# Casting x in a cross-attention kernel: reading in order and writing into two halves in turn, against reading at a step of two columns

## The chip, the cores and the metric

The kernel runs on one core of one Trainium2 chip. The metric is the device time of one execution in microseconds (us). A core has four compute engines here: PE (matrix products, with weight loads shown apart as PEld), DVE, ACT and POOL. SP issues DMAs. SBUF is the working memory that DMAs fill and all engines read; PE writes its results into eight PSUM banks (the tile `banks`).

## The reference, cut to what matters

```python
B, C, N = (32, 256, 1024)
x_q = jnp.einsum('oc,bcn->bno', w_qk, y)
x_k = jnp.einsum('oc,bcn->bon', w_qk, x)
x_v = jnp.einsum('oc,bcn->bon', w_v, x) + b_v[None, :, None]
energy = jnp.einsum('bnc,bcm->bnm', x_q, x_k)
attention = jax.nn.softmax(energy, axis=-1)
attention = attention / (1e-07 + attention.sum(axis=1, keepdims=True))
x_r = jnp.einsum('bcn,bnm->bcm', x_v, attention)
x_r = jax.nn.relu(jnp.einsum('oc,bcn->bon', w_t, x - x_r) + b_t[None, :, None])
return x + x_r
```

All is float32. For each of 32 batches a 1024 x 1024 score matrix is made, normalised along its rows by the softmax and then along its columns by a sum, and used to mix the values.

## The kernel before, in words

**Three forms.** PE works on operands of type fp32r, a rounded fp32. To keep fp32 precision every operand is held in three forms, HIGH, LOW and REST: HIGH is the value as a cast to fp32r rounds it, REST is what the cast lost, and for x LOW is HIGH / 4096 plus REST. A product of two operands is then three products of like forms, added in a bank. So x becomes `xf`, y becomes `yf`, the key side of the scores becomes `gf`, the softmax rows become `ef` (four buffers in turn), and the values become `uf`. The weights are multiplied together beforehand (`gw`, `vw`, `tw`).

**Layout of the moving operand.** A row of 1024 columns of `xf`, `gf` or `ef` is stored in two halves: the first 512 places hold the even columns, the other 512 the odd ones. PE reads its moving operand through `woven` (L275): element 0 of the first half, element 0 of the second, element 1 of the first, and so on, so that columns come in their natural order. `parted` (L278) views a row as [2 halves][512], `in_turn` (L284) views a row in natural order as [even or odd][512], at a step of two columns.

**Loading x (`load_x`, L372).** For each of the two blocks of 128 channels of a batch: SP's DMA brings x into `xr` in natural order; ACT casts it into `xf` HIGH; POOL subtracts HIGH from `xr` into REST; ACT scales HIGH into LOW; POOL's DMA adds REST to LOW. The first batch has its own code (`first_x`, four casts of 512 columns) and is not touched by the change. So `load_x` runs for 31 batches and issues 62 casts; the profile shows them as ACT `CAST xf<-xr 128x1024`.

**One batch.** Eight row tiles of scores (`energy`, L494, tokens E0 to E7): PE makes a 128x1024 tile in a pair of banks from `yf` and `gf` (shown as `MATMUL banks<-gf,yf`, twelve to a tile, six for each half of 512 columns); DVE takes the row's minimum (`TENSOR_REDUCE small<-banks`), ACT the exponential in the banks, DVE the reciprocal of the row's sum; then for each half of 512 columns ACT scales the row into `ef` HIGH (`ACTIVATE ef<-banks,small`), DVE makes REST (`SCALAR_TENSOR_TENSOR ef<-banks,small,ef`) and DVE adds the row to the running column sums `acc`. Only then may PE write that half of the pair again. ACT and POOL make LOW. `attention` (L549, tokens A0 to A7) multiplies `uf` by `ef` into four banks kept for the whole batch, again twelve products. Around them stand the values of the batch (V, v), the product of x with w_t (W), the keys of the next batch (k), the column sums (S), the output (O), the loads of y (Y) and `load_x` of the next batch (X).

**What sets the order.** The tokens of a batch stand in strings written by hand, for the steady batches

```python
STEADY = (
    "W0^ E0^ E1 E2 W1^ V1^ E3 Y2 A0 E4 A1 E5 A2 X E6 A3 E7 Y3 S A4 A5 v0 k1 A6 A7 k0 O"
)
```

They fix PE's order. For the other engines a planner (`Plan`, L19) estimates a cost and a due time for every instruction (for ACT: `columns / 1200 + 0.1` us, L243) and orders each engine's queue by them before the kernel is built; an engine then works through its queue strictly in that order. An instruction's cost in the plan depends on its number of columns alone, not on how they are read or written.

Of the kernel before, what the change touches and what calls it, by code (L numbers as in the profile page):

```python
# [184 lines left out]
def kernel(  # L185
# [12 lines left out]
    B, C, N = x.shape  # L198
# [12 lines left out]
    HIGH, LOW, REST = range(FORMS)  # L211
# [24 lines left out]
    pe, dve, act, pool, sync = (InOrder(g) for g in (nc.tensor, nc.vector, nc.scalar, nc.gpsimd, nc.sync))  # L236
# [6 lines left out]
    def on_act(columns, reads, writes, trace, more=0.0):  # L243
        plan.add("act", columns / 1200 + 0.1 + more, 0.09, reads, writes, trace)
# [11 lines left out]
    def on_pool(columns, reads, writes, trace):  # L256
        busy = columns * 2.25 / 1024 + 0.12
        plan.add("pool", busy, 0.0, reads, writes, trace, port=busy)

    def by_sync(landing, reads, writes, trace, early=0.0):  # L260
        plan.add("sync", 0.4, landing, reads, writes, trace, early=early)
# [4 lines left out]
    def by_pool(landing, reads, writes, trace):  # L266
        plan.add("pool", 1.2, landing, reads, writes, trace)

    def value(v):
        return v.bitcast(F32)  # L270
# [7 lines left out]
    def parted(v):  # L278
        return v.rearrange("p (a b) -> p a b", a=2)
# [4 lines left out]
    def in_turn(v):  # L284
        return v.rearrange("p (b a) -> p a b", a=2)

    def accumulate(into, from_):
        pool.dma_start(into, from_, accum_op=ALU.add)
# [9 lines left out]
    xf = one.tile([P, FORMS, KC, N], F32R, name="xf")  # L298
# [4 lines left out]
    xr = one.tile([P, KC, N], F32, name="xr")  # L303
# [65 lines left out]
    def x_names(j, k, halves=range(MH)):  # L369
        return [f"xf{j}{k}{h}" for h in halves]  # L370

    def load_x(b):  # L372
        for k in range(KC):

            def of(k=k):
                raw = [f"xr{k}{h}" for h in range(MH)]
                by_sync(5.0, ["yr"] if b == 1 else [], raw, lambda: sync.dma_start(xr[:, k], x[b, ts(k, P)]))
                on_act(N, raw, x_names(HIGH, k), lambda: act.copy(parted(xf[:, HIGH, k]), in_turn(xr[:, k])))
                on_pool(
                    N, raw + x_names(HIGH, k), x_names(REST, k),  # L380
                    lambda: pool.tensor_tensor(
                        parted(xf[:, REST, k]), in_turn(xr[:, k]), parted(value(xf[:, HIGH, k])), ALU.subtract
                    ),
                )
                on_act(
                    N, x_names(HIGH, k), x_names(LOW, k),
                    lambda: act.mul(xf[:, LOW, k], value(xf[:, HIGH, k]), 1.0 / UP),
                )
                by_pool(
                    8.2, x_names(LOW, k) + x_names(REST, k), x_names(LOW, k),  # L390
                    lambda: accumulate(value(xf[:, LOW, k]), value(xf[:, REST, k])),
                )

            of()
# [572 lines left out]
```

## Time and profile before

| what | value |
|---|---|
| median of three runs | 1881.09 us (1876.34 to 1881.65) |
| the profiled execution's own time | 1882.61 us |
| span of its instructions | 1880.7 us |
| mean granted TensorE clock | 0.998 |
| the 62 casts of x on ACT | 93.6 us of ACT's 1484.8 us |

The profile is of one execution. A row of the groups shows an instruction's output and inputs by the program's tile names, the shape, the count, then the busy time in us and the mean of one in ns, and the idle time of its engine just ahead of it with what ended that. All instructions have line 231, the helper that records them, so they are told apart by tiles. A row of a timeline shows the start in us, the time that the merged row takes, the engine and instruction, how many there are (x), and in brackets the idle time before it. Consecutive instructions of an engine overlap a little at their ends. A row of the waits shows the total in us, how often, and the longest.

### The profile page before, as it was taken

Reading aid. Unit: us, or ns where it says so; the run is one execution under the profiler, and the core shown is the slowest. Engines: PE = TensorE matmul, PEld = TensorE weight load, DVE = VectorE, ACT = ScalarE, POOL = GpSimd, SP = SyncE. Lnnn points to the kernel's source line nnn. Section 1 sums busy time; section 2 is a strip of 40 time slices with the busy share of each in tenths; the row PEclk is TensorE's granted clock in tenths of the full one; section 3 lists DMA queues with packets and bytes.
Section 4 is the critical chain, followed back from the end, with each engine's and each line's share of the span. In section 5 each row is a group of like instructions: output and inputs, shape, how many; then the busy total and the mean of one; then the engine's idle time right before and its main releaser. Section 6 shows DMA issues by size and latency. Waiting matters only on the chain.

```text
span 1880.7 us, 24352 instructions
## 1 busy us (share of the span) xinstructions
PE 1855.6 (99%) x8494; PEld 1597.4 (85%) x8494; DVE 1493.0 (79%) x2106; ACT 1484.8 (79%) x1936; POOL 1541.4 (82%) x773
## 2 busy tenths in 40 slices
PE   8999999999999999999999999999999999999998
PEld 7888888888888888888888888888888888888887
DVE  6787777887778878878777787777887877877878
ACT  6788777897777987778877789777797777887775
POOL 4788888888788888788888888888888788888777
PEclk9999999999999999999999999999999999999999
DMA  6666766667667667666676666666767666667652
GB/s 187 137 154 169 178 157 157 162 163 178 160 154 170 154 183 173 152 153 162 167 180 157 157 160 165 175 160 152 174 152 184 169 154 151 170 165 177 150 119 79
DMA packets 128651, 301.88 MB, mean 161 GB/s; under 512 B 12688, under 2 KB 47120, under 8 KB 128528
## 3 DMA queue, kind: packets, MB, share of 16 engines
q1 hardware_dynamic: 92272, 200.45, 34.4%
q0 software_dynamic: 35680, 99.10, 31.0%
q8 instruction: 66, 1.08, 0.2%
q10 hardware_dynamic: 576, 0.79, 0.1%
q14 instruction: 57, 0.47, 0.1%
HBM read 167.38 MB, written 67.11 MB: 125 GB/s over the span
## 4 chain that ended last, share of the span: by engine, by line
PE 33%; ACT 28%; DVE 14%; DMA 11%; issue 8%; POOL 4%; SPq 1%; DVEq 0%; POOLq 0%; ACTq 0%
PE banks L231 33%; ACT ef L231 10%; DMA blocks<-turned 6%; ACT banks L231 5%; DVE ef L231 5%; ACT xf L231 5%; DMA yr<-blocks 4%; DVE acc L231 4%; ACT xe L231 3%; ACT uf L231 3%; POOL ef L231 2%; DVE small L231 2%; ACT z L231 1%; SPq L231 1%; DVE parts L231 1%
## 5 line engine op out<-in xcount | busy, mean ns | idle before, releaser
L231 PE MATMUL banks<-gf,yf 128*128 128x512 f32 x3072 | 705.5, 381 | 8.5 <-DMA yf<-yf 2.8
L231 POOL TENSOR_TENSOR ef<-ef 128x1024 fp32r<-128x1024 f32 x256 | 640.5, 2516 | 79.8 <-DVE acc L231 35.4
L231 PE MATMUL banks<-ef,uf 128*128 128x512 f32 x3072 | 694.7, 379 | 1.1 <-POOL ef L231 0.6
L231 PEld LDWEIGHTS banks<-gf,yf 128*128 128x128 f32 x3072 | 576.2, 189 | 107.5 <-DVE ef L231 24.9
L231 PEld LDWEIGHTS banks<-ef,uf 128*128 128x128 f32 x3072 | 580.2, 189 | 85.1 <-POOL ef L231 1.4
L231 DVE TENSOR_REDUCE small<-banks 128x1 f32<-128x1024 f32 x256 | 312.5, 1221 | 174.1 <-PE banks L231 174.1
L231 DVE SCALAR_TENSOR_TENSOR ef<-banks,small,ef 128x512 fp32r<-128x512 f32 x512 | 366.5, 742 | 48.5 <-ACT ef L231 47.6
L231 ACT ACTIVATE ef<-banks,small 128x512 fp32r<-128x512 f32 x512 | 335.5, 706 | 4.1 <-DVE acc L231 0.6
L231 DVE SCALAR_TENSOR_TENSOR acc<-banks,small,acc 128x512 f32<-128x512 f32 x448 | 319.6, 743 | 5.7
L231 ACT ACTIVATE banks<-banks,small 128x1024 f32<-128x1024 f32 x256 | 281.8, 1101 | 23.2 <-DVE small L231 23.0
L231 ACT ACTIVATE ef<-ef 128x1024 fp32r<-128x1024 f32 x256 | 276.7, 1081 | 1.2
L231 ACT ACTIVATE gf<-banks 128x1024 fp32r<-128x1024 f32 x64 | 65.4, 1023 | 261.7 <-PE banks L231 259.8
L231 POOL TENSOR_TENSOR z<-z,xe 128x1024 f32<-128x1024 f32 (+1 forms) x64 | 149.1, 2345 | 68.2 <-DVE z L231 65.7
L231 POOL TENSOR_TENSOR uf<-yr,uf 128x1024 fp32r<-128x1024 f32 x64 | 152.2, 2377 | 57.4 <-ACT uf L231 57.1
L231 PE MATMUL banks<-xf,vw 128*128 128x512 f32 x768 | 183.4, 383 | 7.5 <-DVE ef L231 6.7
L231 PE MATMUL banks<-xf,gw 128*128 128x512 f32 x768 | 177.3, 380 | 1.1 <-DVE xf L231 0.7
L231 PE MATMUL banks<-xf,tw 128*128 128x512 f32 x774 | 176.5, 378 | 0.9 <-DVE banks L231 0.9
L231 PEld LDWEIGHTS banks<-xf,vw 128*128 128x128 f32 x768 | 142.6, 189 | 38.2 <-DVE ef L231 19.2
L231 PEld LDWEIGHTS banks<-xf,gw 128*128 128x128 f32 x768 | 144.7, 189 | 23.5 <-ACT acc L231 1.1
L231 PEld LDWEIGHTS banks<-xf,tw 128*128 128x128 f32 x774 | 145.4, 189 | 22.1 <-DVE banks L231 1.3
L231 POOL TENSOR_TENSOR uf<-turned,uf 128x1024 fp32r<-128x1024 f32 x64 | 154.9, 2420 | 8.5 <-ACT uf L231 6.2
L231 POOL TENSOR_TENSOR xf<-xr,xf 128x1024 fp32r<-128x1024 f32 x62 | 149.3, 2429 | 1.0 <-ACT xf L231 1.0
(68 smaller groups left out, 1633.8 us busy)
## 6 DMA issues: line engine op xcount, KB each, us to landing
yr<-in_ctx_dram SPq DMA_DIRECT2D x64, 512.0 KB, 4.3
blocks<-turned SPq DMA_DIRECT2D x256, 128.0 KB, 3.2
yf<-in_ctx_dram POOLq DMA_DIRECT2D x63, 512.0 KB, 6.1
yf<-yf POOLq DMA_DIRECT2D x63, 512.0 KB, 7.4
xo<-in_x_dram SPq DMA_DIRECT2D x62, 512.0 KB, 4.4
xr<-in_x_dram SPq DMA_DIRECT2D x62, 512.0 KB, 4.8
xf<-xf POOLq DMA_DIRECT2D x62, 512.0 KB, 6.7
out_dram<-z SPq DMA_DIRECT2D x62, 512.0 KB, 4.1
```

Source lines behind the costliest of these rows:

```text
L231: self.last = getattr(self.engine, name)(*args, **kwargs)
```

## The change

The cast into `xf` HIGH in `load_x` keeps its source, its destination and its 1024 columns, and visits them in another order. Before, it goes through the first half of the destination and then the second, contiguous in writing, and reads every other column of `xr`. After, it reads `xr` column by column and writes them to the first half and the second half in turn, so that each write is 512 places away from the one before. Both sides of the instruction become [512][2] where they were [2][512]. POOL's subtraction behind it, the set-up's casts and the plan are as they were.

```diff
                 by_sync(5.0, ["yr"] if b == 1 else [], raw, lambda: sync.dma_start(xr[:, k], x[b, ts(k, P)]))
-                on_act(N, raw, x_names(HIGH, k), lambda: act.copy(parted(xf[:, HIGH, k]), in_turn(xr[:, k])))
+                on_act(N, raw, x_names(HIGH, k), lambda: act.copy(
+                    xf[:, HIGH, k].rearrange("p (a b) -> p b a", a=2), xr[:, k].rearrange("p (b a) -> p b a", a=2)
+                ))
                 on_pool(
```

## The prediction

> **What bounds the kernel now.** I read the page of the profile first, then ACT's groups by shape, the waits, and last the timeline of each engine around one pair of the casts that the change edits.
>
> ```profile
> span 1880.7 us, 24352 instructions
> ...
> PE 1855.6 (99%) x8494; PEld 1597.4 (85%) x8494; DVE 1493.0 (79%) x2106; ACT 1484.8 (79%) x1936; POOL 1541.4 (82%) x773
> ```
>
> PE is busy 99% of the span, so the end moves only if PE does less or stands still less. The change takes nothing from PE's work. The question is whether ACT, through this cast, makes PE stand still. PE's waits name one large releaser:
>
> ```profile
> PEld banks L231 <- DVE ef L231: 44.8, 100, 1.6
> ...
> PE banks L231 <- DVE ef L231: 8.6, 17, 1.2
> ```
>
> These are a hundred short waits of PE's weight loads on DVE's step of the softmax, some three in each of 32 batches. One of the three is tied to the cast. This is the timeline of one batch in the middle, first ACT, then DVE, then PE with its weight load:
>
> ```profile
> 797.87 0.68 ACT L231 ACTIVATE ef<-banks,small 128x512 fp32r<-128x512 f32 x1
> 798.43 3.02 ACT L231 CAST xf<-xr 128x1024 fp32r<-128x1024 f32 x2
> 801.36 0.68 ACT L231 ACTIVATE ef<-banks,small 128x512 fp32r<-128x512 f32 x1
> 801.95 1.08 ACT L231 ACTIVATE banks<-banks,small 128x1024 f32<-128x1024 f32 x1
> ```
> ```profile
> 795.88 0.15 DVE L231 RECIPROCAL small<-small 128x1 f32<-128x1 f32 x1
> ...
> 799.83 1.22 DVE L231 TENSOR_REDUCE small<-banks 128x1 f32<-128x1024 f32 x1
> 802.08 0.75 DVE L231 SCALAR_TENSOR_TENSOR ef<-banks,small,ef 128x512 fp32r<-128x512 f32 x1 [1.04 <-ACT ef L231]
> ```
> ```profile
> 798.71 2.75 PE L231 MATMUL banks<-ef,uf 128*128 128x512 f32 x12
> 801.30 3.15 PE L231 MATMUL banks<-gf,yf 128*128 128x512 f32 x12
> 804.29 2.75 PE L231 MATMUL banks<-ef,uf 128*128 128x512 f32 x12
> 806.88 2.75 PE L231 MATMUL banks<-gf,yf 128*128 128x512 f32 x12
> ```
> ```profile
> 802.89 1.16 PEld L231 LDWEIGHTS banks<-gf,yf 128*128 128x128 f32 x6 [0.53 <-DVE ef L231]
> ```
>
> Read it backwards. A group of twelve products usually shows 2.75 us; the one from 801.30 shows 3.15, because its second six had to wait: 0.53 us in the weight loads, of which 3.15 - 2.75 = 0.40 us is lost on PE. They waited for DVE's ef at 802.08 to 802.83, which reads the bank that they overwrite. DVE had been idle 1.04 us, waiting for ACT's ef of 801.36. That ef is the second half of a tile whose first half ran at 797.87; the reciprocal that both need was there at 796.03. Between the halves stand the two casts, 3.02 us, on an engine that had no gap. So the chain is: two casts, ACT ef, DVE ef, PE.
>
> The rows repeat in the same form from the second batch that loads to the last but one:
>
> ```profile
> 105.37 3.02 ACT L231 CAST xf<-xr 128x1024 fp32r<-128x1024 f32 x2
> ...
> 1725.13 3.02 ACT L231 CAST xf<-xr 128x1024 fp32r<-128x1024 f32 x2
> ```
> ```profile
> 109.82 1.16 PEld L231 LDWEIGHTS banks<-gf,yf 128*128 128x128 f32 x6 [0.53 <-DVE ef L231]
> ...
> 1729.58 1.16 PEld L231 LDWEIGHTS banks<-gf,yf 128*128 128x128 f32 x6 [0.53 <-DVE ef L231]
> ```
>
> These are the first and the last of 29. The first and the last loading batch have another order.
>
> **The change part by part.** One instruction is edited, issued 62 times, two to a batch that loads. Plan, order, queues and DMAs stay. Only the duration of the cast can change, on its read side and on its write side.
>
> *What the strided read costs now.* ACT's groups by shape (count, then busy time and mean ns of one):
>
> ```profile
> L231 ACT CAST xf<-xr 128x1024 fp32r<-128x1024 f32 x62 | 93.6, 1555 | 0.0
> ...
> L231 ACT CAST yf<-yr 128x1024 fp32r<-128x1024 f32 x64 | 69.4, 1084 | 0.0
> ...
> L231 ACT ACTIVATE gf<-banks 128x1024 fp32r<-128x1024 f32 x64 | 65.4, 1023 | 261.7 <-PE banks L231 259.8 <-DVE sc L231 1.9
> ...
> L231 ACT CAST uf<-turned 128x1024 fp32r<-128x1024 f32 x32 | 33.9, 1060 | 0.7 <-DMA turned<-blocks 0.7
> ```
>
> The cast of x takes 1555 ns, casts of the same size that read in order 1084 and 1060. So reading SBUF at a step of two costs about 0.49 us. It is not the step alone: gf reads the PSUM banks at the same step in 1023 ns. Nor does the step cost as much when PE is quiet. In the set-up the cast in halves takes 725 ns beside 614 for a half in order, 0.11 more instead of the 0.25 that half of 0.49 would be; and in the first batch one full cast falls on a pause of PE and takes 1.34:
>
> ```profile
> L231 ACT CAST xf<-xr 128x512 fp32r<-128x512 f32 x4 | 2.7, 725 | 0.0
> L231 ACT ACTIVATE yf<-yf 128x512 fp32r<-128x512 f32 x3 | 1.7, 614 | 0.0
> ```
> ```profile
> 48.10 1.41 DVE L231 SCALAR_TENSOR_TENSOR ef<-banks,small,ef 128x512 fp32r<-128x512 f32 x2 [0.27 <-ACT ef L231]
> 48.53 1.34 ACT L231 CAST xf<-xr 128x1024 fp32r<-128x1024 f32 x1
> 48.90 3.10 PEld L231 LDWEIGHTS banks<-gf,yf 128*128 128x128 f32 x15 [0.59 <-DVE ef L231]
> 48.91 3.29 PE L231 MATMUL banks<-gf,yf 128*128 128x512 f32 x14 [0.18 <-DVE ef L231]
> ```
>
> I take the extra 0.49 us to be the strided read beside PE's reads of SBUF. The edit removes it, since the new read is in order.
>
> *What the scattered write will cost.* No ACT row of the trace writes SBUF element by element into two places. The lower bound is the 1060 ns of the uf cast, which writes in runs of 64; below the 1023 of gf I see no reason to go. For the upper bound the nearest rows are DVE's small sums: the first reads and writes at a step of five columns, the second is in order.
>
> ```profile
> L231 DVE TENSOR_REDUCE parts<-parts 32x32 f32<-32x32 f32 x96 | 19.7, 205 | 1.9
> ...
> L231 DVE TENSOR_REDUCE sc<-sc 32x32 f32<-32x32 f32 x32 | 5.6, 175 | 1.1
> ```
>
> That is 30 ns more for 32 elements, 0.94 ns an element. Laid wholly on the write of 1024 elements it gives 1.06 + 0.96 = 2.02 us. So the new cast lies between 1.06 and 2.02 us. I take 1.06, for two reasons. First, what slowed the read was PE reading beside it, and every product of PE writes into banks, never into SBUF: on the write side PE is no rival. Second, PE itself takes its moving operand from the two halves in turn, element by element, with the very step of the new write, and the timeline above shows no price: groups of twelve start 2.59 us apart (804.29 and 806.88), 216 ns for 512 columns.
>
> The Trainium skill has a rule that speaks against this change: "SBUF — State Buffer", section Specifications (TRN2), says that SBUF is kept in 16-byte lines, that full bandwidth needs at least two hits to a line, and that each step to a new line costs. By it the old read (two fp32 columns to a line) should be free and the new write (a new line at each element) should pay; the trace disagrees on the first (1555 against 1084) and, for PE's reads, on the second (216 ns at a new line for each column). The page gives no size, so the sum by it is the slower rival below.
>
> *What becomes of the time.* With 1.06 each, the two casts shorten by 2 x (1.555 - 1.06) = 0.99 us. ACT's ef moves up by as much, DVE's ef too, since DVE sat idle 1.04 us before it; PE needs only 0.53 of it. What is late next: DVE's TENSOR_REDUCE ends at 801.05, so its ef could end at 801.80, and PE reaches its second six products at about 802.6 (801.30 + 6 x 0.216). No stall is left there; half of the gain is unused. POOL does not see it: its own queue holds the next use of xf until 800.40.
>
> ```profile
> 798.05 2.40 POOL L231 TENSOR_TENSOR ef<-ef 128x1024 fp32r<-128x1024 f32 x1 [0.86 <-ACT ef L231]
> 800.40 4.81 POOL L231 TENSOR_TENSOR xf<-xr,xf 128x1024 fp32r<-128x1024 f32 x2
> ```
>
> The sum: 29 x 0.40 = 11.6 us. In the first loading batch DVE waited 0.27 us for an ef behind a single cast (48.10, above) and PE for DVE: 0.27. In the last one POOL waited 0.23 us for the cast and PE later 0.44 for POOL: 0.23.
>
> ```profile
> 1780.53 2.42 POOL L231 TENSOR_TENSOR xf<-xr,xf 128x1024 fp32r<-128x1024 f32 x1 [0.23 <-ACT xf L231]
> ...
> 1787.69 1.13 PE L231 MATMUL banks<-ef,uf 128*128 128x512 f32 x4 [0.44 <-POOL ef L231]
> ```
>
> Together 12.1 us. The profiled execution took 1882.6 us, so 1870.5; the median of the three runs lies 1.5 below the profiled time, so 1869.0. The other stalls of PE on DVE's ef come before the cast in each batch, from a chain that starts at PE's own products, and I leave them as they are.
>
> **The rivals.** *Slower: the write pays more than the read saves.* The place is the same; the point from which it decides is a cast of 1.555 us. Above it the stall grows by twice the excess in each batch, without slack, since ACT, DVE and PE already wait for each other in a row there. At 2.02 us: 29 x 2 x 0.465 = 27.0, and about 1 more in the two other batches, so 1881.1 + 28 = 1909. For it: DVE's strided small sums, and that a write of single elements into two places can't be gathered into wider ones. The page's rule on lines asks for this outcome. Against it: PE's reads in turn. Chance 0.33.
>
> *No change.* Either the price moves from the read to the write and the cast stays within 0.09 us of 1.555 (62 x 0.09 = 5.6 us, the bound of 0.3%), or the instruction pays for its inner run of two elements on both sides; or PE's gap stays although ACT is early. Against the last: DVE's idle 1.04 us ends with ACT's ef and nothing else. About 1881. Chance 0.13.
>
> *Faster*, as summed: any cast below about 1.30 us gives the whole 12 us, since 0.5 us for the pair is enough. Chance 0.54.
>
> **How the numbers follow.** The forecast is 1869.0. A difference of 0.3% (5.6 us) is about what a measurement of this kernel can tell from no change; the three runs spread over 5.3 us. The low end is the fastest of them less the gain, 1876.3 - 12.1 = 1864. Faster and no change hold 0.67, so the range must reach into the slower case, to its worked end of 1909 and a little over: 1912. The likeliest case's own range is 1864 to 1873. Faster 0.54, same 0.13, slower 0.33.
>
> **What would show it.** Right: the group of the cast near 1.06 us; the pair on ACT's timeline 2.0 instead of 3.02; DVE's ef behind it without its 1.04 of idle time; the group of twelve after it 2.75 instead of 3.15; PE's waits on DVE's ef down from 100 by about 29, and by 29 x 0.53 = 15 us. Wrong: a cast of 1.6 us or more, with DVE's idle time before ef longer and PE's group over 3.15; or a cast near 1.06 and the span unmoved, which would mean that another wait took the stall's place.

## The result, and the profile after

The changed kernel takes 1901.54 us (median of 4 runs, 1899.08 to 1905.83), the kernel before 1878.71 (median of 4 runs, the three shown and one more): a ratio of 1.0124 with a 95% interval of 1.0094 to 1.0155. It is slower, by about 23 us. The profiled executions differ by as much: 1905.83 against 1882.61 us.

The groups of ACT by shape show the edited instruction first (count, busy us, mean ns, idle time before it):

```profile
L231 ACT CAST xf<-xr 128x1024 fp32r<-128x1024 f32 x62 | 122.5, 2080 | 0.0
L231 ACT CAST yf<-yr 128x1024 fp32r<-128x1024 f32 x64 | 70.2, 1097 | 0.0
```

The cast takes 2080 ns where it took 1555, while the other casts are within 2% of what they were. The edit did what it says, and it cost 0.53 us a cast. These are the timelines of ACT, DVE, PE and PE's weight loads around one pair of casts, to be read as before from the bottom up:

```profile
866.98 0.69 ACT L231 ACTIVATE ef<-banks,small 128x512 fp32r<-128x512 f32 x1
867.55 3.94 ACT L231 CAST xf<-xr 128x1024 fp32r<-128x1024 f32 x2
871.27 0.68 ACT L231 ACTIVATE ef<-banks,small 128x512 fp32r<-128x512 f32 x1
871.84 1.09 ACT L231 ACTIVATE banks<-banks,small 128x1024 f32<-128x1024 f32 x1
```
```profile
868.95 1.22 DVE L231 TENSOR_REDUCE small<-banks 128x1 f32<-128x1024 f32 x1
871.98 0.75 DVE L231 SCALAR_TENSOR_TENSOR ef<-banks,small,ef 128x512 fp32r<-128x512 f32 x1 [1.82 <-ACT ef L231]
```
```profile
867.83 2.75 PE L231 MATMUL banks<-ef,uf 128*128 128x512 f32 x12
870.42 1.46 PE L231 MATMUL banks<-gf,yf 128*128 128x512 f32 x6
872.79 1.56 PE L231 MATMUL banks<-gf,yf 128*128 128x512 f32 x6 [0.92 <-DVE ef L231]
874.19 2.75 PE L231 MATMUL banks<-ef,uf 128*128 128x512 f32 x12
```
```profile
872.79 1.16 PEld L231 LDWEIGHTS banks<-gf,yf 128*128 128x128 f32 x6 [1.32 <-DVE ef L231]
```

It is the same chain. ACT's second half of the ef tile starts 871.27 - 867.55 = 3.72 us after the first cast; before it was 801.36 - 798.43 = 2.93. DVE's idle time before its ef rose from 1.04 to 1.82, the weight loads' wait from 0.53 to 1.32. PE's group starts 870.42 and the next one 874.19, 3.77 us apart instead of the 2.99 of before (801.30 to 804.29). Each of these moved by 0.78 or 0.79 us. It is the sign that the prediction named for being wrong: a cast above 1.6 us, a longer idle time of DVE before its ef, and more than 3.15 us for PE's group. Over the span, PE's waits on DVE's ef grew from 44.8 and 8.6 us to

```profile
PEld banks L231 <- DVE ef L231: 67.9, 101, 1.7
...
PE banks L231 <- DVE ef L231: 36.2, 45, 1.3
```

To add up what PE loses, I took from the trace the start of every product and counted what two neighbours are further apart than 0.216 us, if it is over 0.05 us, in the 29 batches with a pair of casts: from the first cast of a batch to 12 us after it ("behind the pair"), and in the 12 us ahead of the next pair. The table has the sums in us, with all kernels of this study; the last six are explained further down.

```
kernel               behind the pair   ahead of the next   time, median us
before                    11.5               12.4             1879.2
changed                   34.6               12.7             1901.5
one of two changed        22.6               12.9             1891.0
in order on both sides     0.0               12.5             1869.7
runs of two                0.0               12.7             1869.4
runs of eight              0.0               12.3             1869.3
half moved up, before      7.0               14.7             1879.0
half moved up, changed    31.4               12.5             1904.0
```

The change added 34.6 - 11.5 = 23.1 us behind the pairs. Over the whole execution the same count gives 41.9 us before and 65.2 us after, 23.3 more, so nothing worth naming was added elsewhere. That is the whole loss.

### The profile page after: what moved, and what is told of

Read it like the earlier page. It is cut to its first block, busy times and chain, and to the rows that moved or that the text cites. A ratio compares the mean times of both kernels' runs of the same rounds, so it can differ in the third digit from the quotient of the medians.

```text
span 1904.1 us, 24352 instructions
## 1 busy us (share of the span) xinstructions
PE 1854.6 (97%) x8494; PEld 1597.0 (84%) x8494; DVE 1493.3 (78%) x2106; ACT 1510.7 (79%) x1936; POOL 1547.3 (81%) x773
## 4 chain that ended last, share of the span: by engine, by line
PE 41%; ACT 25%; DVE 13%; DMA 9%; issue 8%; POOL 3%; SPq 1%; DVEq 0%; POOLq 0%; ACTq 0%
PE banks L231 41%; ACT ef L231 9%; ACT banks L231 5%; DMA blocks<-turned 5%; ACT xf L231 4%; DVE ef L231 4%; DVE acc L231 4%; DMA yr<-blocks 3%; ACT xe L231 3%; DVE small L231 2%; ACT uf L231 2%; POOL ef L231 1%; DVE parts L231 1%; ACT z L231 1%; SPq L231 1%
## 5 line engine op out<-in xcount | busy, mean ns | idle before, releaser
L231 ACT ACTIVATE gf<-banks 128x1024 fp32r<-128x1024 f32 x64 | 65.5, 1024 | 261.8 <-PE banks L231 259.9
```

The source lines that it names most:

```text
L231: self.last = getattr(self.engine, name)(*args, **kwargs)
```

## The experiments

My theory after the result: the write in turn itself is dear for ACT, and each of the two casts stretches the chain of ACT, DVE and PE without slack. The first rival: it is PE's reading that makes the write dear, as I had argued for the read. The second: the place of the casts in ACT's queue is at fault, not their length.

**The casts alone.** A kernel without the attention, which lets ACT cast one block eight ways, six times each, with PE quiet and beside two kinds of PE products:

```diff
+    ways = {
+        "plain": (lambda v: v, lambda v: v),
+        "rd2": (lambda v: v.rearrange("p (a b) -> p a b", a=2), lambda v: v.rearrange("p (b a) -> p a b", a=2)),
+        "wr_turn": (halves_out, lambda v: v.rearrange("p (b a) -> p b a", a=2)),
...
+            for _ in range(TIMES):
+                act.do("copy", to(into), from_(xr))
```

> This kernel leaves the attention out: it loads one block of 128x1024 of x and lets ACT cast it eight ways, six times each, first with PE quiet, then beside PE products whose moving operand is read from two halves in turn (turn), then beside products that read it in order (row). Ways: in order on both sides (plain), read at a step of two (rd2, the cast before), written into the two halves in turn (wr_turn, the cast after), read from two halves in turn and written in order (rd_turn), written at a step of two (wr2), and reads at a step of two with writes in runs of 2, 4 and 16 columns. Theory W, the write itself pays: wr_turn near 2.0 us in all three stages, rd_turn near 1.1, runs of 4 and 16 no dearer than rd2. Theory P, only PE's traffic makes it dear: wr_turn and rd2 near 1.1 with PE quiet, near 2.0 and 1.55 beside PE. Theory I, an inner run of two elements pays on either side: wr_turn, rd_turn and the runs of 2 all near 2.0. For the strided read, from the row of the first batch: near 1.1 to 1.3 with PE quiet, 1.55 beside it. All three expect 1.06 for plain in every stage.

The groups of ACT (the tile names show the stage and the way, with their numbers left out, so that the three lengths of run share a row):

```profile
L31 ACT CAST turn_run<-xr 128x1024 fp32r<-128x1024 f32 x18 | 20.4, 1143 | 0.5
...
L31 ACT CAST quiet_run<-xr 128x1024 fp32r<-128x1024 f32 x18 | 19.9, 1114 | 0.5
L31 ACT CAST row_wr_turn<-xr 128x1024 fp32r<-128x1024 f32 x6 | 12.4, 2070 | 0.2
L31 ACT CAST turn_wr_turn<-xr 128x1024 fp32r<-128x1024 f32 x6 | 12.1, 2023 | 0.2
L31 ACT CAST quiet_wr_turn<-xr 128x1024 fp32r<-128x1024 f32 x6 | 11.8, 1959 | 0.2
L31 ACT CAST turn_rd<-xr 128x1024 fp32r<-128x1024 f32 x6 | 9.4, 1569 | 0.2
...
L31 ACT CAST quiet_rd_turn<-xr 128x1024 fp32r<-128x1024 f32 x6 | 7.6, 1273 | 0.2
...
L31 ACT CAST row_rd<-xr 128x1024 fp32r<-128x1024 f32 x6 | 6.7, 1109 | 0.2
L31 ACT CAST quiet_rd<-xr 128x1024 fp32r<-128x1024 f32 x6 | 6.6, 1108 | 0.2
```

Theory W holds: the write in turn takes 1.96 us with PE quiet and 2.02 to 2.07 beside it, so it is the write and not PE. Theory P falls for the write in turn, but it holds for the old cast: the read at a step of two takes 1.11 us with PE quiet, 1.11 beside products that read in order, and 1.57 only beside products that read two halves in turn, as this kernel's do. The same holds for a write at a step of two: 1.10 us with PE quiet, 1.12 and 1.56 beside the two kinds of products. Theory I falls: reading in turn costs 1.27 (more than the 1.1 that all but theory I gave it, but far from 2.0), and runs of two, four and sixteen columns take 1.11 to 1.14 in every stage on the mean of the three lengths, and 1.10 to 1.16 each by itself. These runs were the surprise, since these casts also read at a step of two and write into both halves.

**One of two casts changed.**

```diff
-                ))
+                ) if k == 0 else act.copy(parted(xf[:, HIGH, k]), in_turn(xr[:, k])))
```

> Only the first of a batch's two casts is written in turn, the second is as before. Theory: the chain of cast, cast, ACT ef, DVE ef, PE has no slack, so half of the whole change's 22.8 us is lost, about 1890, and PE's stall behind the pair is about 0.8 us where it was 0.40 before and 1.19 after. Rival: the loss comes from what else the longer cast disturbs (POOL's subtraction behind the first cast), then it would be all or nothing: near 1879 or near 1901.

1890.99 us, ratio 1.0063 (1.0043 to 1.0084), about half of the whole change's loss. The pair on ACT's timeline takes 3.40 us, between 3.02 and 3.94, and PE lost 22.6 us behind the pairs, half way from 11.5 to 34.6:

```profile
806.86 3.40 ACT L231 CAST xf<-xr 128x1024 fp32r<-128x1024 f32 x2
```

So the chain passes on each cast's length by itself, and no threshold shows between the two.

**The cast in order on both sides.**

```diff
-act.copy(parted(xf[:, HIGH, k]), in_turn(xr[:, k]))
+act.copy(xf[:, HIGH, k], xr[:, k])
```

> The cast reads and writes in order, so that the columns of the HIGH form of x are left in natural order, and not in halves of even and odd columns; everything else is the kernel before. It gives the cast that the prediction counted on. Theory: cast 1.06 us, no stall of PE behind the pair, 12 us below before, about 1867. Rival: another wait takes the stall's place and the time stays near 1879.

POOL's subtraction is unchanged, so REST takes up the difference to the unsorted HIGH. The time is 1869.68 us, ratio 0.9944 (0.9927 to 0.9961). The cast takes 1055 ns, and behind the pairs PE loses nothing any more:

```profile
L231 ACT CAST xf<-xr 128x1024 fp32r<-128x1024 f32 x62 | 62.1, 1055 | 0.0
```

So the prediction's way from a shorter cast to a shorter time was right. What it had wrong is the cast that this edit gives.

**The half of the tile moved up, in the changed kernel.** The emitted list is edited so that the second ACT ef goes further to the front; the queues of all other engines are as they were. It was meant to go in front of the pair. The timeline below shows that the edit moves it by one cast only: in all 29 batches it stands between the two casts.

```diff
+        at = ops.index(cast)
+        behind = [op for op in ops[at + 1 :] if op.engine == "act"][:2]
+        late = [op for op in behind if op.writes[0][:2] == "ef" and len(op.writes) == 1][:1]
+        for op in late:
+            if all(ops.index(o) < at for o in op.needs.values()):
+                out.insert(at, out.pop(ops.index(op)))
```

> The changed kernel with its slow cast, and one edit in ACT's queue: the second half of the ef tile goes ahead of the two casts instead of behind them. No other engine's order changes. Theory: the loss is the place of the casts between the two halves; with the half ahead of them PE's stall there goes, and the time is at or below that of before, 1867 to 1875, though the cast still takes 2.08 us. Rival: the 0.8 us more of ACT's time per batch comes back at the next tile, whose exponential then waits, and the time stays near 1900.

The theory of this run, the second rival above, fell and its own rival came true: 1904.01 us, ratio 1.0127 (1.0111 to 1.0142), nothing gained. ACT, DVE and PE of one batch:

```profile
864.71 0.69 ACT L231 ACTIVATE ef<-banks,small 128x512 fp32r<-128x512 f32 x1
865.28 2.07 ACT L231 CAST xf<-xr 128x1024 fp32r<-128x1024 f32 x1
867.13 0.69 ACT L231 ACTIVATE ef<-banks,small 128x512 fp32r<-128x512 f32 x1
867.70 2.09 ACT L231 CAST xf<-xr 128x1024 fp32r<-128x1024 f32 x1
869.54 1.16 ACT L231 ACTIVATE banks<-banks,small 128x1024 f32<-128x1024 f32 x1
```
```profile
870.85 0.16 DVE L231 RECIPROCAL small<-small 128x1 f32<-128x1 f32 x1 [2.25 <-ACT banks L231]
```
```profile
868.14 2.75 PE L231 MATMUL banks<-gf,yf 128*128 128x512 f32 x12
870.73 2.75 PE L231 MATMUL banks<-ef,uf 128*128 128x512 f32 x12
874.30 2.86 PE L231 MATMUL banks<-gf,yf 128*128 128x512 f32 x12 [0.81 <-DVE ef L231]
```

One cast still stands between the halves, but the second half starts 867.13 - 865.28 = 1.85 us after the first cast instead of 3.72. The group at 868.14 no longer stands still, but the next group of scores does, for 874.30 - 870.73 - 2.59 = 0.98 us. The next tile's exponential stands behind both casts as it did: it starts 869.54 - 865.28 = 4.26 us after the first cast began, and 871.84 - 867.55 = 4.29 without this edit. DVE waits 2.25 us for it, and PE for DVE. So the loss is not due to the half alone. In this stretch ACT has no gap, and PE needs both the half and the next exponential soon after; what the casts take longer is paid with the half in either place. A queue with the exponential ahead of the casts, or the half ahead of both, was not tried.

**The same edit in the kernel before.**

> The kernel before, with the second half of the ef tile put ahead of the two casts in ACT's queue. In the changed kernel this moved PE's stall to the next tile, whose exponential now waited behind the casts, and gave nothing. Theory: ACT's whole run of work from the first half to the next tile's exponential is the chain, so the order inside it does not matter: the stall is again about as large one tile later, and the time is 1877 to 1882. Rival: with the shorter cast the next tile has slack enough, and the time falls by up to 12 us.

1879.04 us, ratio 1.0001 (0.9992 to 1.0010). Here too the half stands between the two casts in all 29 batches. The theory as mended holds as far as it was tried: where the half stands does not matter for the time. One thing stays open. The trace of this kernel has 7.0 us behind the pairs instead of 11.5, and 2.3 us more ahead of the next; the 2 us that this leaves do not show in the times.

**What makes the write dear.** A second kernel without the attention, with steps of two to four columns on either side, and writes in turn into two areas that lie side by side:

```diff
+        "write_three": (3, step(3), plain),
+        "write_four": (4, step(4), plain),
+        "write_near": (1, lambda v: v.rearrange("p (c a b) -> p c b a", a=2, b=32), plain_near),
...
+        "read_four": (1, plain, lambda v: step(4)(v)),
```

> The attention is left out again: ACT casts 128x1024 columns six times each, with PE quiet and then beside PE products that read two halves in turn: in order, written at a step of two, three and four columns, written in turn into two blocks of 32 columns that lie side by side (near), and read at a step of two, three and four. At the end DVE copies in order and in turn, with all else quiet. Theory L, what counts is how many elements in a row fall into one line of 16 bytes: write_two stays near 1.1 with PE quiet, write_three lies between, write_four and write_near cost as much as the write in turn, 1.96; the same for the reads, if they pay at all. Theory D, the far jump of 512 columns is what pays: write_near and write_four stay near 1.1. DVE: by L its copy in turn is slower than in order too, if its port has the same lines; else the same.

```profile
L31 ACT CAST turn_write_four<-wide 128x1024 fp32r<-128x1024 f32 x6 | 17.7, 2953 | 0.2
L31 ACT CAST turn_read_four<-wide 128x1024 fp32r<-128x1024 f32 x6 | 17.7, 2944 | 0.2
...
L31 ACT CAST quiet_read_four<-wide 128x1024 fp32r<-128x1024 f32 x6 | 11.9, 1987 | 0.2
L31 ACT CAST quiet_write_four<-wide 128x1024 fp32r<-128x1024 f32 x6 | 11.9, 1985 | 0.2
L31 ACT CAST quiet_write_near<-wide 128x1024 fp32r<-128x1024 f32 x6 | 11.8, 1958 | 0.2
L31 ACT CAST turn_write_two<-wide 128x1024 fp32r<-128x1024 f32 x6 | 9.4, 1562 | 0.2
...
L31 ACT CAST quiet_write_three<-wide 128x1024 fp32r<-128x1024 f32 x6 | 9.3, 1547 | 0.2
...
L31 ACT CAST quiet_write_two<-wide 128x1024 fp32r<-128x1024 f32 x6 | 6.6, 1104 | 0.2
L31 ACT CAST quiet_plain<-wide 128x1024 fp32r<-128x1024 f32 x6 | 6.3, 1044 | 5.2 <-DMA wide<-in_x_dram 5.0
```

With PE quiet the writes take 1.10, 1.55 and 1.99 us at a step of two, three and four columns: 0.44 more for each column of step. A step of four puts each fp32 element 16 bytes from the last, and costs what the write in turn costs, near (1.96) or far (1.96 in the first probe). So the distance of the jump does not matter. What fits all writes with PE quiet, theory L, is the number of elements in a row that fall into one line of 16 bytes: two are nearly free, one costs 0.9 us, and at a step of three, where half of the elements share their line with a neighbour, the price lies half way. The reads at a step follow the same numbers, but the read in turn of the first probe does not: each of its elements is far from the last, and it takes 1.27 us and not 1.99. So for reads the account is incomplete. Theory D falls. DVE's copies at the end take 692 ns in order and 1078 in turn: its price for the same write is 0.39 us, against ACT's 0.92. Whether that has the same cause is not shown.

**Runs of two.** The probe's surprise, put into the kernel before: the cast takes four columns of x at a time and writes two to each half.

```diff
-act.copy(parted(xf[:, HIGH, k]), in_turn(xr[:, k]))
+act.copy(
+    xf[:, HIGH, k].rearrange("p (a c d) -> p c a d", a=2, d=2),
+    xr[:, k].rearrange("p (c d a) -> p c a d", a=2, d=2),
+)
```

> The kernel before, with the cast visiting four columns of x at a time: the two even ones go to the first half, then the two odd ones to the second, so that it writes two columns in a row before it jumps. From the probe the cast takes about 1.13 us beside PE. Theory: the pair shortens by about 0.85 us, which is more than the 0.5 that the stall needs, so the whole stall goes, as with the cast in order on both sides: about 1869 to 1870, ratio 0.994 to 0.995. Rival: in the full kernel, beside POOL, DVE and the DMAs, a run of two is no better than the strided read, and the time stays near 1880.

1869.41 us, ratio 0.9951 (0.9939 to 0.9964): faster than both kernels, and every value still goes to the place that it had. ACT's group, and the timelines of ACT, DVE and PE at a pair:

```profile
L231 ACT CAST xf<-xr 128x1024 fp32r<-128x1024 f32 x62 | 68.6, 1167 | 0.0
```
```profile
793.11 2.20 ACT L231 CAST xf<-xr 128x1024 fp32r<-128x1024 f32 x2
795.17 0.71 ACT L231 ACTIVATE ef<-banks,small 128x512 fp32r<-128x512 f32 x1
```
```profile
795.91 0.75 DVE L231 SCALAR_TENSOR_TENSOR ef<-banks,small,ef 128x512 fp32r<-128x512 f32 x1 [0.19 <-ACT ef L231]
```
```profile
795.97 2.75 PE L231 MATMUL banks<-gf,yf 128*128 128x512 f32 x12
798.56 2.75 PE L231 MATMUL banks<-ef,uf 128*128 128x512 f32 x12
```

The pair takes 2.20 us, DVE still waits 0.19, and PE's group shows its usual 2.75. PE's weight loads now wait for DVE's ef 72 times instead of 100:

```profile
PEld banks L231 <- DVE ef L231: 29.2, 72, 1.5
```

**Runs of eight.** The same with `d=8`.

> The same with sixteen columns of x at a time and runs of eight. Theory: 1.13 to 1.15 us for the cast, the stall gone, the same 1869 to 1870 as with runs of two, since only the half microsecond that the stall needs counts. Rival: if every further lengthening of the runs gave time, it would be below runs of two by 2 us or more.

1869.30 us, ratio 0.9949 (0.9937 to 0.9961), a cast of 1175 ns. Longer runs give nothing more, in the cast or in the time. Nor does a still shorter cast: the one in order on both sides, at 1055 ns, gave 1869.68. The stall is gone, and no one waits for the rest of the shortening, as the theory has it.

## Why the prediction was wrong

- **The bound and the chain: right.** PE stood still behind each pair of casts, by way of ACT's ef and DVE's ef. The stall moved with the cast, up by 0.79 us a batch in the changed kernel, half of that with one cast, to nothing with casts in order or in runs.
- **The strided read costs 0.49 us and it is PE's reading beside it: right.** Alone it costs 0.06 us (1.108 against the 1.044 of a cast in order), and beside PE's reads from two halves 0.53. Beside products that read in order it costs no more than alone (1.109).
- **"I take 1.06": this step failed.** The measured 2.08 us lies just over the upper of the bounds, 1.06 and 2.02. I took the lower one for two reasons, and neither carried. That PE writes nothing into SBUF does not keep it from disturbing ACT's writes: a write at a step of two takes 1.10 us with PE quiet and 1.56 beside reads in turn. And the write in turn needs no rival; it costs 1.96 us with PE quiet. That PE reads two halves in turn at full rate says nothing of ACT: ACT's own read in turn costs 1.27 and its write 1.96. I carried a row over from another engine and from reading to writing. That the upper bound came so near is luck. It too came from another engine, from DVE's small sums, and gave 0.96 us for the write in turn, where DVE itself pays 0.39.
- **The slower rival: right in place and mechanism, and a little too large.** It had a loss of 28 us, up to 1909; the loss is 22.8, up to 1901.5. Its term was 2 x 0.465 = 0.93 us a batch from the casts' durations. What counts is how long a cast holds ACT's queue: from the first cast to the ef behind the pair it was 2.93 us and is 3.72, so 0.79, though two durations grew by 1.05. Neighbours overlap more when the cast is slow: two of 2.08 take 3.94 together. 29 x 0.79 = 22.9 us, the measured loss.
- **The rule that spoke against the change.** The Trainium skill, "SBUF — State Buffer", section Specifications (TRN2), with its 16-byte lines and two hits to a line, was right on ACT's write; the steps of two to four columns and the runs of two agree with a line of that size. ACT's read in turn does not agree: it goes to a new line at each element and took 1.27 us, where a step of four took 1.99. I set the rule aside because two rows seemed to contradict it. One of them (1555 ns for the old read) shows PE's disturbance and not the line, as the quiet row of 1108 shows. The other is PE's own reading, and there the trace of the first probe still speaks against the rule: products that read in turn stood 0.216 us apart, those that read in order 0.233. But that does not carry over to ACT.
- **The sum of the faster case: right in mechanism, a little too large.** It had 12.1 us; casts in order gave 1879.6 - 1869.7 = 9.9 and runs of two 9.8, though their traces show all of the 11.5 us behind the pairs gone. The 2 us between can be noise: the interval of 0.9927 to 0.9961 with casts in order stands for a gain of 7.3 to 13.7 us.

## What to carry to other kernels

When an access must be strided on one side, do not choose between a strided read and a scattered write alone: a walk in small blocks, which keeps two fp32 elements in a row on the write side and comes back to the same source columns at once, cost a tenth of a microsecond where the two simple orders cost half and one. A price between wide bounds belongs to the row of the same engine and the same side; without such a row, a rule that speaks against the change deserves more weight than a likeness to another engine. And where an engine has no gap and another waits for several results of its run of work, bringing one of them forward can do no more than move the wait, as it did here.

## What the hardware showed beside this

ACT is not undisturbed by PE. Beside products that read two halves in turn, a step of two columns rose from 1.10 to 1.56 us and a step of four from 1.99 to 2.95, on the read and on the write side alike, while casts in order, casts in short runs and the write in turn hardly moved (1.044 in both stages, 1.114 to 1.143, and 1.96 to 2.02). Why the runs are spared, though they too read at a step of two, was not tried further.

PE itself reads faster in turn than in order. These are the two stages of the first probe:

```profile
L31 PE MATMUL banks<-moving,w_row 128*128 128x512 f32 x480 | 112.3, 396 | 0.5 <-ACT w_row L31 0.5
L31 PE MATMUL banks<-moving,w_turn 128*128 128x512 f32 x479 | 105.2, 383 | 0.0
```

That is 112.3 / 480 = 0.234 us a product in order against 105.2 / 479 = 0.220 in turn. The second figure holds a slow beginning of the stage, nine products that start 0.37 to 0.59 us apart; behind them the products in turn start 0.216 us apart, and those in order 0.233. It speaks for this kernel's layout in halves, which no run here has replaced.
